# Graph layer on one core: the last node blocks in a new order with any PSUM bank, and the kept units' gathers one in 30 units

## The chip, the cores and the metric

The kernel runs on one core of one Trainium2 chip. The core has five engines with a queue each: TensorE (PE, matmuls into PSUM), VectorE (DVE), ScalarE (ACT), GpSimd (POOL) and SyncE (SP, which here only issues DMAs). The metric is the device time of one execution in microseconds. The kernel before took 2141.97 us as the median of three runs (2139.69 to 2142.32). One more execution was profiled: it took 2142.29 us, and all times of the trace below are of that one. PSUM has eight banks; the kernel calls them pz0 to pz7, and one holds 128 x 512 numbers.

## The reference

A graph layer on 6,250 nodes of 256 features and 206,250 edges of 64 features, sorted by their target node:

```
h    = relu(layernorm(x))                                  # one row per node
e    = relu(raw @ W_e1.T + b_e1) @ W_e2.T + b_e2           # one row per edge
emb  = (e * (clip(pol, 0, 1) + 0.01)) @ W_le.T + b_le
aggr = segment_sum(relu(h[src] + emb), dst)
g    = (h + aggr) @ W_g1.T + b_g1
out  = x + relu(layernorm(g) * ln_g + ln_b) @ W_g2.T + b_g2
```

## The kernel before, in words

**Edges.** W_e2 and W_le are multiplied into one matrix at the start. The edges go in 403 blocks of 512. A block is two *units* of 256 edges, 806 in all (0 to 805), and six blocks are a *group*: 12 units, 68 groups, the last of one block. For one unit PE makes the product with the second matrix (L369) in a bank that ACT has filled with the bias (L399). DVE multiplies by the polarity and adds the gathered rows of h (L754, two instructions), ACT takes the ReLU (L765), and PE sums the rows by target node with a 0/1 matrix as weights (L802). The first layer of a whole group (L335) is made in one stretch after the group's predecessor's last unit: twelve products through the banks, evicted by ACT (L350) and DVE (L347). The sums of a group gather in one bank and are copied to SBUF as `ms` (L820, L822).

**Gathers.** The rows of h come from DRAM by two indirect DMAs for each unit, which POOL issues (L721) into a ring of 25 places. Units 0 to 23 are *kept*: their products were made while h was being computed, and wait in SBUF as `msg`. For units 4 to 23 the gathers are made later and stand between those of other units: `EVERY` (L47) and L705 to L708 say where. Before, unit r's two gathers are ahead of those of unit 24 + 24 (r - 3), so at units 48, 72 and so on to 504. When all 12 units of a kept group have their rows, the group is summed at the end of the running group (24 `msg` matmuls, from `ready` in `add_pairs`, L848), and two node blocks can follow.

**Nodes.** The 6,250 rows are 49 blocks of 128. A block whose groups are done is turned (L173), multiplied by W_g1 (`first`, L188, with the bias added by DVE at L196 or, with `bias_by_pe`, by a one-row matmul, L186), normalised (statistics L158 and L159, square root on ACT L202, reciprocal and scaling L207 and L208), turned again with ReLU on ACT (`second`, L214 and L218), multiplied by W_g2 (`third`, L227), added to x (L232) and stored (L235: SP, and for a last block of 106 rows 10 rows from ACT's queue). Most blocks run beside the edges, a step every unit or two, in a bank that the edges do not use (`Banks.__call__`, L294: `take(False, False)` asks for a bank that last held node work). The sums of groups go to the blocks either through DRAM (`rows_out`, SP, then `far_work`) or, for blocks at the end, by selecting matmuls (L1026, L1045: `node_work`).

**End.** Five blocks are left when the last edge is done. `ending[-2]` (*held*, 128 rows) and `ending[-1]` (the *last*, 106 rows) need the last groups. Three more, the *fillers* (`held_back`, `far_work(..., True)`, L840), could be done before: their rows are summed (L942), but all six steps (`turned`, `one`, `rooted`, `normed`, `two`, `three`) wait for the end, where L1139 to L1168 write the order out by hand. Every engine works its queue in order, so this order decides what waits behind what. A clock gate on PE shows in the profile as the granted clock.

Of the kernel before, what the change touches and what calls it, by code (L numbers as in the profile page):

```python
# [29 lines left out]
L = 6  # L30
# [5 lines left out]
NG = NF + 1  # L36
# [6 lines left out]
RAW = 4  # L43
# [3 lines left out]
EVERY = 24  # L47
SEEDS = 3
FILL = 3
# [51 lines left out]
def gnn_kernel(ctx: ExitStack, tc: tile.TileContext, x, src_c, dst_c, dst_r, pol_c, raw_t, w_e1t, w_e2,  # L101
# [149 lines left out]
    with fast:  # L251
# [22 lines left out]
        class Banks:  # L274

            def __init__(self):
                self.all = [Bank(psz.tile([P, 2, D], F32, name=f"pz{i}")) for i in range(BANKS)]
                self.uses = 0

# [14 lines left out]
            def __call__(self):  # L294
                self.now = self.take(False, False) or self.take(False)
                self.now.reader = self.now.writer = None
                return self.now.tile
# [397 lines left out]
        with tc.tile_pool(name="hg", bufs=1) as hg_p, tc.tile_pool(name="ms", bufs=4) as ms_p, \  # L695
# [9 lines left out]
            for r in range(RAW, KEPT):  # L705
                i = KEPT + EVERY * (r - RAW + 1)
                beside[i] = r
                order.insert(order.index(i), r)  # L708
# [218 lines left out]
            def far_work(w, nd=nd, nh=nh, ab_p=ab_p, filling=False):  # L927
# [37 lines left out]
                def run(i):  # L965
                    stages[i]()
                    if i < len(stages) - 1:
                        at(now + (2, 1, 1, 2, 3)[i], lambda: run(i + 1))
# [5 lines left out]
                if filling:  # L974
                    fillers.append(stages)
                else:
                    at(now + 12, lambda: run(0))
# [10 lines left out]
            def node_work(w, spread_now=False):  # L988
# [82 lines left out]
                ending[gs[-1] - NG].append((sums_of, halves_out, rows_of, one, two, three, gs))  # L1071
# [67 lines left out]
            (held, held_out, held_rows, h_one, h_two, h_three, _), = ending[-2]  # L1139
            (sums_of, halves_out, rows_of, one, two, three, gs), = ending[-1]  # L1140
            f = fillers
            for i in range(FILL):
                f[i][0]()
            held_rows()
            sums_of(gs[:-1])
            add_pairs(last=True)
            f[0][1]()
            h_one()
            sums_of(gs[-1:])
            halves_out()  # L1150
            f[1][1]()
            one()
            for i in range(2):
                f[i][2]()
                f[i][3]()
            f[0][4]()
            h_two()
            f[2][1]()
            f[1][4]()
            f[2][2]()  # L1160
            f[0][5]()
            two()
            f[2][3]()
            h_three()
            f[1][5]()
            three()
            f[2][4]()
            f[2][5]()  # L1168
# [184 lines left out]
```

## Time and profile before

| | us |
|---|---|
| median of three runs | 2141.97 |
| the profiled execution, time | 2142.29 |
| its span, first to last instruction | 2140.6 |
| PE busy | 2095.3 (98%) |
| POOL busy | 1574.8 (74%) |
| DVE busy, ACT busy | 1305.4, 1296.9 (61% each) |
| mean granted clock of PE | 0.994 |

The profile puts 1.69 us of the time outside the span. PE is the engine that is busy nearly throughout; POOL's busy share leaves out the pause between two gathers. In a timeline row stand the start, the length, the engine, the line, the operation with its tiles, the number of instructions merged, and in brackets the idle time ahead of the row and what ended it. The trace counts every float32 matmul of the program twice.

### The profile page before, as it was taken

Reading aid. Unit: us, or ns where it says so; the run is one execution under the profiler, and the core shown is the slowest. Engines: PE = TensorE matmul, PEld = TensorE weight load, DVE = VectorE, ACT = ScalarE, POOL = GpSimd, SP = SyncE. Lnnn points to the kernel's source line nnn. Section 1 sums busy time; section 2 is a strip of 40 time slices with the busy share of each in tenths; the row PEclk is TensorE's granted clock in tenths of the full one; section 3 lists DMA queues with packets and bytes.
Section 4 is the critical chain, followed back from the end, with each engine's and each line's share of the span. In section 5 each row is a group of like instructions: output and inputs, shape, how many; then the busy total and the mean of one; then the engine's idle time right before and its main releaser. Section 6 shows DMA issues by size and latency. Waiting matters only on the chain. (4 is left out here: it accounts for less than half of the span.)

```text
span 2140.6 us, 35567 instructions
## 1 busy us (share of the span) xinstructions
PE 2095.3 (98%) x11940; PEld 1568.3 (73%) x11940; DVE 1305.4 (61%) x2867; ACT 1296.9 (61%) x2392; POOL 1574.8 (74%) x1675
## 2 busy tenths in 40 slices
PE   9999999999999999999999999999999999999997
PEld 6676777677778767777767777777777777777775
DVE  7766566565656666656566565566665666656563
ACT  7655566566656656656656565656665666666662
POOL 6777777777777777777777777777777777777760
PEclk9999999999999999999999999999999999999998
DMA  9545455555555554555555455555455555554550
GB/s 318 192 140 159 147 152 159 148 153 149 158 151 158 155 153 142 158 152 152 154 152 164 136 159 151 161 163 159 142 160 151 158 151 160 157 153 132 155 147 13
DMA packets 143653, 330.48 MB, mean 154 GB/s; under 512 B 35999, under 2 KB 71416, under 8 KB 142712
## 3 DMA queue, kind: packets, MB, share of 16 engines
q0 software_dynamic: 77376, 211.39, 34.5%
q1 hardware_dynamic: 64788, 113.47, 16.4%
q10 hardware_dynamic: 1300, 3.28, 0.4%
q8 instruction: 96, 1.57, 0.3%
q14 instruction: 93, 0.76, 0.1%
HBM read 306.24 MB, written 34.08 MB: 159 GB/s over the span
## 5 line engine op out<-in xcount | busy, mean ns | idle before, releaser
L721 POOL DMA_INDIRECT hg<-hb_d,src_s x1348 | 1286.9, 955 | 412.8 <-issue 246.2
L369 PE MATMUL pz<-wc_s,e 128*128 128x256 f32 x6448 | 1440.9, 380 | 0.2 <-ACT pz L399 0.2
L369 PEld LDWEIGHTS pz<-wc_s,e 128*128 128x128 f32 x6448 | 1212.0, 190 | 189.8 <-issue 28.7
L754 DVE SCALAR_TENSOR_TENSOR hg<-pz,pol_s,hg 128x256 f32<-128x256 f32 x1348 | 594.9, 480 | 593.9 <-PE pz L369 261.1
L765 ACT ACTIVATE hg<-hg 128x512 f32<-128x512 f32 x673 | 423.4, 629 | 502.4 <-DVE hg L754 498.2
L399 ACT ACTIVATE pz<-bc_s 128x512 f32<-128x512 f32 x782 | 453.0, 586 | 0.0
L335 PE MATMUL pz<-raw,we_s 64*128 64x512 f32 x1612 | 381.8, 609 | 25.0 <-DVE hg L754 15.1
L347 DVE TENSOR_SCALAR e<-pz,vecs 128x512 f32<-128x512 f32 x395 | 292.3, 750 | 57.2 <-PE pz L335 25.0
L335 PEld LDWEIGHTS pz<-raw,we_s 64*128 64x128 f32 x1612 | 147.3, 188 | 223.5 <-issue 118.6
L721 POOL DMA_INDIRECT hx<-hb_d,src_s x256 | 243.0, 949 | 78.0 <-issue 52.4
L350 ACT ACTIVATE e<-pz,vecs 128x512 f32<-128x512 f32 x411 | 269.9, 682 | 40.8 <-PE pz L335 35.9
L802 PE MATMUL pz<-hg,sel 128*32 128x256 f32 x2696 | 167.0, 381 | 1.0 <-ACT ms L820 1.0
L802 PEld LDWEIGHTS pz<-hg,sel 128*32 128x32 f32 x2696 | 84.4, 110 | 96.2 <-ACT e L350 44.2
L754 DVE SCALAR_TENSOR_TENSOR hx<-pz,pol_s,hx 128x256 f32<-128x256 f32 x216 | 95.3, 480 | 94.3 <-PE pz L369 36.6
L765 ACT ACTIVATE hx<-hx 128x512 f32<-128x512 f32 x108 | 68.0, 630 | 100.1 <-DVE hx L754 99.9
L736 DVE SCALAR_TENSOR_TENSOR sel<-iota_w,zero_c,rel 128x256 f32<-128x256 f32 x202 | 97.1, 481 | 46.2 <-PE pz L802 46.2
L820 ACT ACTIVATE ms<-pz 128x256 f32<-128x256 f32 x67 | 25.7, 383 | 146.5 <-PE pz L802 144.4
L188 PE MATMUL pz<-wg_s,hT 128*128 128x256 f32 (+1 forms) x176 | 46.5, 387 | 0.0
L227 PE MATMUL pz<-wg_s,nT 128*128 128x256 f32 (+1 forms) x176 | 45.6, 382 | 0.0
L523 POOL TENSOR_TENSOR hb<-xt,rows_b 128x256 f32<-128x256 f32 (+1 forms) x49 | 34.1, 727 | 9.7 <-issue 2.6
L188 PEld LDWEIGHTS pz<-wg_s,hT 128*128 128x128 f32 (+1 forms) x176 | 33.4, 192 | 6.2 <-issue 1.0
L227 PEld LDWEIGHTS pz<-wg_s,nT 128*128 128x128 f32 (+1 forms) x176 | 33.5, 192 | 5.0 <-ACT hT L177 0.4
(135 smaller groups left out, 605.6 us busy)
## 6 DMA issues: line engine op xcount, KB each, us to landing
raw<-in_raw_t_dram SPq DMA_DIRECT2D x99, 512.0 KB
hg<-hb_d,src_s POOLq DMA_INDIRECT x1348
sum_d<-zero_d SPq DMA_DIRECT2D x47, 256.0 KB
ab<-sum_d SPq DMA_DIRECT2D x42, 256.0 KB
sum_d<-ms SPq DMA_DIRECT2D x264, 32.0 KB
hb_d<-hb SPq DMA_DIRECT2D x12, 512.0 KB
xt<-in_x_dram SPq DMA_DIRECT2D x11, 512.0 KB
xt<-in_x_dram SPq DMA_DIRECT2D x43, 128.0 KB
```

The source lines that it names most:

```text
L188: z = nc.tensor.matmul(ph[:n, 0, :], aT[:, c, :n], wg1_s[:, c, :], start=c == 0 and not bias_by_pe, stop=c == 1)
L227: z = nc.tensor.matmul(po[:n, 0, :], nT[:, c, :n], wg2_s[:, c, :], start=c == 0, stop=c == 1)
L335: z[c] = nc.tensor.matmul(bank[s, c].tile.rearrange("p a b -> p (a b)"), we1_s[s * F:(s + 1) * F, c * P:(c + 1) * P], raw[q][s * F:(s + 1) ...
L347: a = nc.vector.tensor_scalar(e1[b][:, c, :], pe, be1_s[:, c:c + 1], 0.0, op0=ALU.add, op1=ALU.max)
L350: a = nc.scalar.activation(e1[b][:, c, :], pe, AF.Relu, bias=be1_s[:, c:c + 1])
L369: z = nc.tensor.matmul(bank.tile[:, i, :], e1[b][:, c, k:k + P], wc_s[:, c, :], start=not seeded and i == c == 0, stop=c == 1, skip_group_ ...
L399: a = nc.scalar.activation(bank.tile, bc_s, AF.Copy)
L721: g = nc.gpsimd.indirect_dma_start(out=hg[u][:, i, :], out_offset=None, in_=hb_d, in_offset=bass.IndirectOffsetOnAxis(ap=src_s[:, 2 * u + ...
L736: nc.vector.scalar_tensor_tensor(sel[g][:, k * S:k * S + n, :], iota_w.rearrange("p (o w) -> p o w", o=1).to_broadcast([P, n, W]), zero_c, ...
L754: product = nc.vector.scalar_tensor_tensor(hg[u][:, i, :], bank.tile[:, i, :], pol_s[:, 2 * u + i:2 * u + i + 1], hg[u][:, i, :], op0=ALU. ...
L765: done[u] = product, nc.scalar.activation(hg[u], hg[u], AF.Relu)
L802: z = nc.tensor.matmul(acc[g][j * W:(j + 1) * W, :], sel[g][:, k * S + j, :], m[:, j % 2, :], start=k == 0, stop=b == blocks_of(g)[-1])
```

## The change

Four things are changed.

1. `EVERY` is 30, and unit r's gathers stand ahead of unit 24 + 30 (r - 4) + 15: at units 39, 69 and so on to 609.
2. The fillers run their first four steps beside the edges, like other blocks; only `two` and `three` are held back.
3. At the end any free bank serves node work (`ps.any`), the one free for longest first.
4. The end's order is written anew. The held block's bias is added by DVE instead of PE, and `one` and the normalising are separate steps, so that the two blocks' can be interleaved.

```diff
-EVERY = 24
+EVERY = 5 * L
...
             def __call__(self):
-                self.now = self.take(False, False) or self.take(False)
+                self.now = None if self.any else self.take(False, False)
+                self.now = self.now or self.take(False)
...
-                i = KEPT + EVERY * (r - RAW + 1)
+                i = KEPT + EVERY * (r - RAW) + EVERY // 2
...
-                    if i < len(stages) - 1:
+                    if i < len(stages) - (3 if filling else 1):
...
                 if filling:
-                    fillers.append(stages)
-                else:
-                    at(now + 12, lambda: run(0))
+                    fillers.append(stages[-2:])
+                at(now + 12, lambda: run(0))
...
                 def one():
-                    box["hs"] = scaled(root(first(box["hT"], gs[-1] >= NG - 2)))
+                    box["hs"] = first(box["hT"], gs[-1] == NG - 1)
+                    if gs[-1] < NG - 2:
+                        normed()
...
+                def normed():
+                    box["hs"] = scaled(root(box["hs"]))
```

The end before and after, as written (`f` and `fillers` are the three held blocks, `h_` the held block of 128 rows):

```
before                          after
f[0][0]() f[1][0]() f[2][0]()   ps.any = True
held_rows()                     fillers[0][0]()   # two
sums_of(gs[:-1])                fillers[1][0]()
add_pairs(last=True)            h_rows()
f[0][1]()                       add_pairs(last=True)
h_one()                         sums_of(gs[:-1])
sums_of(gs[-1:])                fillers[2][0]()
halves_out()                    sums_of(gs[-1:])
f[1][1]()                       halves_out()
one()                           h_one()
f[0][2]() f[0][3]()             one()
f[1][2]() f[1][3]()             normed()
f[0][4]()                       fillers[0][1]()   # three
h_two()                         h_normed()
f[2][1]()                       fillers[1][1]()
f[1][4]()                       two()
f[2][2]()                       fillers[2][1]()
f[0][5]()                       three()
two()                           h_two()
f[2][3]()                       h_three()
h_three()
f[1][5]()
three()
f[2][4]() f[2][5]()
```

**PE, behind the last big sum.** These are PE's first rows after the sum of units 800 to 803 before the change: the three fillers' first turns, then the held block's sums, all in bank pz1 (the number behind a tile's name is its buffer).

```order
L173 MATMUL pz1_139<-ident_64,msg7_119 128x128 x2
L173 MATMUL pz1_139<-ident_64,msg15_127 128x128 x2
L173 MATMUL pz1_139<-ident_64,msg23_135 128x128 x2
L1045 MATMUL pz1_139<-s2_14882,ms_14632 128x128
L1045 MATMUL pz1_139<-s2_14884,ms_14842 128x128
```

At the same place after the change the fillers' second turns stand, the held block's sums follow in a bank of their own, and the last unit's sum stands ahead of the last block's.

```order
L214 MATMUL pz1_139<-ident_64,msg5_117 128x128 x2
L214 MATMUL pz7_145<-ident_64,msg13_125 128x128 x2
L1046 MATMUL pz5_143<-s2_14918,ms_14643 128x128
L1046 MATMUL pz5_143<-s2_14920,ms_14864 128x128
L1046 MATMUL pz5_143<-s2_14922,ms_15052 128x128
L1046 MATMUL pz5_143<-s2_14918,ms_14643 128x128
L1046 MATMUL pz5_143<-s2_14920,ms_14864 128x128
L1046 MATMUL pz5_143<-s2_14922,ms_15052 128x128
L804 MATMUL pz6_144<-hg8_819,sel1_137 32x256 x2
L804 MATMUL pz6_144<-hx2_110,sel1_137 32x256 x2
```

The L173 rows have gone up between the edges' products, one block's L173 and L188 about a group apart.

**ACT, at the very end.** Before, these are ACT's last rows: between turns and roots the ten rows of the last block are stored (L235), and one filler's ReLU stands behind that store.

```order
L202 ACTIVATE rs1_15081<-mv1_15077,eps_t_65 106x1
L202 ACTIVATE msg3_115<-msg4_116,eps_t_65 128x1
L202 ACTIVATE msg11_123<-msg12_124,eps_t_65 128x1
L218 ACTIVATE msg3_115<-pz4_142,vecs_167 128x128 x2
L218 ACTIVATE nT_15097<-pz1_139,vecs_167 128x128 x2
L218 ACTIVATE msg11_123<-pz4_142,vecs_167 128x128 x2
L202 ACTIVATE msg19_131<-msg20_132,eps_t_65 128x1
L218 ACTIVATE nT_15116<-pz0_138,vecs_167 128x106 x2
L235 DMA out_0_dram<-ot_15132 10x256
L218 ACTIVATE msg19_131<-pz4_142,vecs_167 128x128 x2
```

After the change the three fillers' ReLUs come first, two roots are left, and the ReLU behind the store is the held block's (nT_15136).

```order
L218 ACTIVATE msg3_115<-pz1_139,vecs_167 128x128 x2
L218 ACTIVATE msg11_123<-pz7_145,vecs_167 128x128 x2
L822 ACTIVATE ms_15073<-pz6_144 128x256
L218 ACTIVATE msg19_131<-pz4_142,vecs_167 128x128 x2
L202 ACTIVATE rs1_15103<-mv1_15099,eps_t_65 106x1
L202 ACTIVATE rs1_15111<-mv1_15091,eps_t_65 128x1
L218 ACTIVATE nT_15121<-pz6_144,vecs_167 128x106 x2
L235 DMA out_0_dram<-ot_15130 10x256
L218 ACTIVATE nT_15136<-pz4_142,vecs_167 128x128 x2
```

**SP, the held block's loads.** Before, on SP's queue x, the turned x and the row statistics of the held block (L240, L999, L1001) stand between the two pairs of stores of group 65's sums (L906).

```order
L906 DMA sum_d_62<-ms_14842 32x256
L240 DMA xt3_14876<-in_x_dram 128x256
L999 DMA hT_14878<-in_x_t_dram 128x2x128
L1001 DMA stb_14880<-st_d_61 128x256
L906 ISA
L906 DMA sum_d_62<-ms_14842 32x256
```

After the change both pairs of stores are ahead of the three loads.

```order
L908 DMA sum_d_62<-ms_14864 32x256
L908 ISA
L908 DMA sum_d_62<-ms_14864 32x256
L240 DMA xt3_14912<-in_x_dram 128x256
L1000 DMA hT_14914<-in_x_t_dram 128x2x128
L1002 DMA stb_14916<-st_d_61 128x256
```

Elsewhere in PE's queue the sum of the second kept group (the rows L802 with msg12 to msg23) stands behind the first layer that follows unit 515 before and unit 611 after; that of the first (msg0 to msg11) behind unit 227 before and 251 after.

More of the change, by code (lines that the diff above doesn't have):

```diff
@@ L278, in __init__ @@
                 self.uses = 0
+                self.any = False
             def take(self, whole, of=None):
@@ L1070, in node_work @@
                     return lambda: at(now + 2, rows_of)
-                ending[gs[-1] - NG].append((sums_of, halves_out, rows_of, one, two, three, gs))
+                ending[gs[-1] - NG].append((sums_of, halves_out, rows_of, one, normed, two, three, gs))
                 return lambda: None
@@ L1138, in gnn_kernel @@
                 steps.popleft()[1]()
[L1139 to L1144, printed above, removed]
+            (_, _, h_rows, h_one, h_normed, h_two, h_three, _), = ending[-2]
+            (sums_of, halves_out, _, one, normed, two, three, gs), = ending[-1]
+            ps.any = True
+            fillers[0][0]()
+            fillers[1][0]()
+            h_rows()
+            add_pairs(last=True)
             sums_of(gs[:-1])
-            add_pairs(last=True)
-            f[0][1]()
-            h_one()
+            fillers[2][0]()
             sums_of(gs[-1:])
             halves_out()
-            f[1][1]()
+            h_one()
             one()
[L1153 to L1156, printed above, removed]
-            h_two()
[L1158 to L1163, printed above, removed]
+            normed()
+            fillers[0][1]()
+            h_normed()
+            fillers[1][1]()
+            two()
+            fillers[2][1]()
+            three()
+            h_two()
             h_three()
[L1165 to L1168, printed above, removed]
         early.close()
```

## The prediction

> **What bounds the kernel now.** I read the page first, then the waits of PE, then the timelines of PE and POOL around those waits, and last the timelines of all engines behind the last edge. PE is busy for 98% of the span, so only its idle time, or a slower clock, can be won. Between 100 and 1440 us its largest wait is this one; between 1460 and 2100 us no wait of L335 is left.
>
> ```profile
> PE pz L335 <- DVE hg L754: 15.1, 12, 2.3
> L721 POOL DMA_INDIRECT hg<-hb_d,src_s x1348: 942/946/2397, 64.5 to 2081.9; - x193
> ```
>
> PE stands at the first layer of a group because DVE has not freed the banks, and DVE waits for gathered rows. The gathers themselves never pause: 946 ns in the median and 0.30 us between them, from the first to the last. Three windows from the first gather count them, and the rows behind them show two stalls and one group without.
>
> ```profile
> 64.00:976.95 912.95, 692.13 (x724) 1.00 0.51 153
> 64.00:1228.47 1164.47, 882.72 (x924) 1.00 0.51 153
> 64.00:1595.74 1531.74, 1161.03 (x1216) 1.00 0.52 154
> ...
> 976.94 0.94 POOL L721 DMA_INDIRECT hg<-hb_d,src_s  x1 [0.30 <-issue]
> 980.36 4.08 PE L335 MATMUL pz<-raw,we_s 64*128 64x512 f32 x16 [2.13 <-DVE hg L754]
> ...
> 1228.46 0.95 POOL L721 DMA_INDIRECT hg<-hb_d,src_s  x1 [0.31 <-issue]
> 1231.75 4.08 PE L335 MATMUL pz<-raw,we_s 64*128 64x512 f32 x16 [1.99 <-DVE hg L754]
> ...
> 1595.74 0.95 POOL L721 DMA_INDIRECT hg<-hb_d,src_s  x1 [0.30 <-issue]
> 1610.59 5.42 PE L335 MATMUL pz<-raw,we_s 64*128 64x512 f32 x24
> ```
>
> Unit 467 ends a group. Its second gather is number 2 x (444 units + 18 kept ones) = 924, issued at 1228.46, and PE goes on 3.3 us later, at 1231.75. For unit 371 it is number 724, and PE goes on 3.4 us later. So PE gets past the first eight matmuls of L335 at the earliest 3.35 us after the last gather of the running group is issued. For unit 611 (588 units and all 20 kept ones, number 1216) that is 1595.74 + 3.35 = 1599.1. PE got there at 1610.59 + 1.99 (the length of eight such matmuls) = 1612.6, so PE was 13.5 us behind the gathers. The first half of the kernel is paced by the gathers, the second by PE.
>
> Then comes the end. The span closes at 2140.6, 37.7 us after the last large sum (start 2101.80, length 1.07). The PE rows behind it:
>
> ```profile
> 2101.80 1.07 PE L802 MATMUL pz<-hx,sel 128*32 128x256 f32 x16
> 2103.42 0.44 PE L173 MATMUL pz<-ident,msg 128*128 128x128 f32 x2 [0.55 <-DVE ms L822]
> ...
> 2106.15 1.60 PE L1045 MATMUL pz<-s,ms 128*128 128x128 f32 x12 [0.47 <-ACT msg L177]
> 2108.34 1.14 PE L1026 MATMUL pz<-s,ms 128*128 128x106 f32 x8 [0.58 <-DVE hT L1047]
> 2109.41 0.64 PE L802 MATMUL pz<-hg,sel 128*32 128x256 f32 x8
> 2110.55 1.13 PE L188 MATMUL pz<-wg_s,msg 128*128 128x256 f32 x4 [0.50 <-ACT ms L820]
> 2112.20 0.69 PE L186 MATMUL pz<-rows_b,ones 1*128 1x256 f32 x2 [0.52 <-DVE msg L196]
> 2112.82 1.13 PE L188 MATMUL pz<-wg_s,hT 128*128 128x256 f32 x4
> 2113.79 0.59 PE L1026 MATMUL pz<-s,ms 128*128 128x106 f32 x4
> 2115.97 2.08 PE L188 MATMUL pz<-wg_s,msg 128*128 128x256 f32 x4 [1.59 <-DVE hT L1034]
> ...
> 2130.64 1.03 PE L227 MATMUL pz<-wg_s,nT 128*106 128x256 f32 x4
> 2131.50 0.38 PE L214 MATMUL pz<-ident,msg 128*128 128x128 f32 x2
> 2133.72 1.13 PE L227 MATMUL pz<-wg_s,msg 128*128 128x256 f32 x4 [1.84 <-ACTq L1173]
> ```
>
> One bank, pz1, carries nearly every step, so each waits for the reader of the one before (0.47 to 0.58 us each), and from 2115.5 the same L188 takes 2.08 us in place of 1.13: the clock was halved, as the windows below show.
>
> **The change, part by part.** Sums are made against the profiled execution, 2142.29 us, which is 0.32 above the median of 2141.97.
>
> *Gathers.* Up to unit 504 there are now 16 kept gathers instead of 20, so PE stalls less there; but the total is the same again from unit 609. The binding place is therefore unit 611, whose gather keeps number 1216 and its time. Against the 13.5 us stands work that PE had done by then and now has not: the second kept group's sum and the two node blocks that follow it. Their rows (the blocks' steps priced where they stand between edges, by the next row's start):
>
> ```profile
> 1361.83 2.80 PE L802 MATMUL pz<-msg,sel 128*32 128x256 f32 x48
> ...
> 1602.51 0.38 PE L214 MATMUL pz<-ident,hs 128*128 128x128 f32 x2
> 1602.72 5.35 PE L369 MATMUL pz<-wc_s,e 128*128 128x256 f32 x24
> 1607.91 1.03 PE L227 MATMUL pz<-wg_s,nT 128*128 128x256 f32 x4
> 1608.77 1.89 PE L369 MATMUL pz<-wc_s,e 128*128 128x256 f32 x8
> ```
>
> A turn costs 0.21 us and a product 0.86, a block 2 x (0.21 + 0.86) = 2.1, together 2.8 + 2 x 2.1 = 7.0. So PE can be at most 13.5 - 7.0 = 6.5 us earlier at unit 611. The other end is that it is not earlier at all, 0. I take 6.0, near the upper end, because at a gather each 1.25 us the ceiling is known to about half a gather. Behind unit 611 the gathers lead by over 10 us, as they did before, so nothing of it is lost later. Loop: -6.0.
>
> *Fillers' first four steps beside the edges.* PE gets three turns and three products more in the loop, 3 x (0.21 + 0.86) = +3.2. Their DVE and ACT work lies in idle time of both engines, which are busy for 61% of the span. It is an addition, statistics, a scaling, a copy and a root, five short instructions of at most 0.54 us (the L208 row below), so without that cover it costs up to 2.7 us a block, 8 in all.
>
> *SP.* The held block's loads go behind two more stores.
>
> ```profile
> 2053.00 0.60 SPq L1001 DMA_DIRECT2D stb<-st_d  x1
> 2057.27 0.33 DVE L1015 SCALAR_TENSOR_TENSOR hT<-hT,zero_c,stb 128x106 f32<-128x106 f32 x1 [3.27 <-DMA stb<-st_d]
> 2076.66 0.60 SPq L1001 DMA_DIRECT2D stb<-st_d  x1
> 2077.57 3.61 SPq L906 DMA_DIRECT2D sum_d<-ms  x2
> ```
>
> Such a load is there 4.3 us after its issue. The held block's was issued at 2076.66. It now follows the second pair of stores, which ended at 2081.2, so it is there about 5 us later than before, and DVE will stand at its first use for some 2 us, with the L754 of units 797 and 798 behind it. The 3.27 us of such a wait above moved no PE row, so I cost it at 0; without that cover it costs those 2 us.
>
> *The end.* I count from the end of the last large sum (0 is 2102.87 before) and lay the new order out with the rows' durations, back to back by the next row's start. PE waits 0.55 for the copy of the sums, since the first turn takes the sum's bank, as before. Then it has, without a wait because ACT and DVE read other banks meanwhile: two turns 0.76, L1045's 12 matmuls 1.53, the last unit's sum 0.57, L1026's eight 1.07, a turn 0.38, L1026's four 0.55, the held block's L188 0.97, L186 0.62, the last block's L188 1.13. That is at 8.1. The last block's chain follows:
>
> ```profile
> 2115.20 0.54 DVE L208 TENSOR_SCALAR hs<-pz,mv,rs 128x256 f32<-128x256 f32 x1
> ...
> 2131.77 0.42 DVE L232 TENSOR_TENSOR ot<-pz,xt 106x256 f32<-106x256 f32 x1 [0.51 <-PE pz L227]
> 2134.89 0.43 DVE L232 TENSOR_TENSOR msg<-pz,msg 128x256 f32<-128x256 f32 x1 [2.70 <-PE pz L227]
> ...
> 2132.86 0.81 ACT L218 ACTIVATE msg<-pz,vecs 128x128 f32<-128x128 f32 x2 [3.25 <-DVE ot L232]
> ```
>
> From L188's end (2113.95) to the end of L208 (2115.74) it took 1.8, so 9.9; turn 0.44, ReLU 0.85 and L227 1.05 bring 12.3, and meanwhile PE makes the fillers' L227, which are free. L232 0.5 ends at 12.8. Behind it ACT's store and a ReLU, L227 and L232 of one more block, the same chain as before though for another block: from 2132.19 to 2135.32, 3.1. Then the last store, to 2140.6: 5.3. The end is 21.2 us long instead of 37.7: -16.5. PE's one-row L186 of the held block goes (0.62) and a DVE addition of 0.42 comes beside PE's work; both are in this count.
>
> Sum: 2142.29 - 6.0 + 3.2 - 16.5 = **2123.0**.
>
> *The clock.* These windows are 3.41 us long and end where the clock changed:
>
> ```profile
> 2101.88:2105.29 3.41, 1.91 (x21) 0.78 (x21) 1.30 (x3) 1.57 (x4) 0.00 (x0) 1.00 0.00 0
> 2112.12:2115.53 3.41, 2.18 (x10) 1.57 (x10) 1.74 (x7) 0.29 (x1) 0.00 (x0) 1.00 0.00 0
> 2115.53:2118.94 3.41, 2.97 (x6) 1.60 (x6) 1.38 (x5) 0.00 (x0) 0.00 (x0) 0.50 0.00 0
> ```
>
> The clock was halved behind a window with 2.18 us of PE work, 0.62 of it the one-row L186, and not behind one with 1.91. Without L186 the shares are 46% and 56%, so I read the limit as about half a window. In the laid-out end PE has a break of 1.8 us ahead of the last L227 (12.5 to 14.3). A window that holds all of it may have 47% of work, and then the last L227 is 1.1 us longer. The Trainium skill (TensorE: Matmul & The Clock Gate, Part 1) has the clock halved after at least one idle window of about 3.4 us, and advises against PE gaps longer than that. By that rule neither end would lose the clock; this trace disagrees, since its clock fell with a longest gap of 1.59 us just before. By the Trainium skill the sum stays 2123.0, by the rows it may be 2124.1.
>
> **The rivals.** *The loop gives nothing* (15%): the stalls between units 39 and 611 come out as long as before, through stalls early (the first kept gather is now at unit 39, not 48) or breaks of the gathers. Then 2129. For it speaks that gathers up to 2397 ns occur; against it the steady 3.35 us. *The clock falls early in the end* (10%), as at 2115.5: from the held sums on about 5.3 us of back-to-back rows and 2.9 in the last chain double: +8.2, 2131. Against it: every 3.41 us window up to 12.5 has over 80% of PE work. *The gathers have fewer long ones* (10%): 1216 gathers at 1.25 us from 64.5 would be issued by 1585, 11 us before 1595.74; half of that would give 2118. *Slower* (3%): the gathers' pace itself is longer. Since it binds at gather 1216, it decides from (19.3 + 4.3) / 1216 = 19 ns a gather on, 1.27 us instead of 1.25, and then the time is above 2146.6; with 25 ns it is 2153. Nothing in the change touches POOL's work, and the median of 946 ns beside a least of 942 speaks against it. That the fillers do not move is ruled out by the order in PE's queue.
>
> **How the numbers follow.** The forecast, 2123.0 with its own range of 2120 to 2126 (1 us for the ceiling, 1.1 for the clock in the last gap, 1 for rounding over some 20 rows), has 62%, the rivals 15, 10, 10 and 3%. A range from 2118 to 2131 holds all but the far ends, some 85 to 90%. A difference of 0.2%, 4.3 us, is about what a measurement of this kernel can tell from none. Faster by more takes all cases but the slower one and some slack for two rivals at once: 0.94; within it 0.03; slower 0.03.
>
> **What would show it.** Right: stalls of L335 until unit 611 (about 1600 us) instead of 515, in sum some 6 us shorter; L173 of the fillers between edges; the last large sum ends near 2100.1; from there 21 us; no half clock ahead of the last L227. Wrong: a wait of PE behind the held block's load, L214 waiting for other than the sum's copy, stalls of L335 behind unit 611, or the clock at 0.5 while the sums run.

## The result and the profile after

The changed kernel takes 2124.28 us (median of 4 runs, 2123.04 to 2124.77), the kernel before 2142.14 (4 runs, 2139.69 to 2148.03): a ratio of 0.9912, with a 95% interval of 0.9891 to 0.9932. The profiled execution took 2124.57 us against 2142.29. The forecast was 2123.0, with a range of 2118 to 2131.

The page of the changed kernel opens with the span and each engine's busy time:

```profile
span 2122.9 us, 35565 instructions
PE 2087.7 (98%) x11938; PEld 1564.9 (74%) x11938; DVE 1303.5 (61%) x2868; ACT 1298.0 (61%) x2392; POOL 1573.9 (74%) x1675
```

The span is 17.7 us shorter and PE is busy for 7.6 us less, though its work is almost the same: in the kernel before, steps of the end ran at half the clock. Two added lines put the names two lines further down, so L335 is L337 here, L721 is L723, L802 is L804.

The waits of PE from 100 to 1700 us in the changed kernel (total, times, longest):

```profile
PE pz L337 <- DVE hg L756: 9.5, 10, 2.0
PE pz L337 <- DVE hx L756: 4.1, 4, 3.2
```

The same two rows said 15.1 and 2.0 before (hx are four more places of the gathers' ring). So the stalls went from 17.1 to 13.6 us, 3.5 less where some 6 were forecast. The last one is now behind unit 611; here is POOL's row of gather 1216, and PE's rows around it:

```profile
1594.57 0.95 POOL L723 DMA_INDIRECT hg<-hb_d,src_s  x1 [0.30 <-issue]
...
1595.59 1.45 PE L337 MATMUL pz<-raw,we_s 64*128 64x512 f32 x6
1597.81 4.08 PE L337 MATMUL pz<-raw,we_s 64*128 64x512 f32 x16 [0.76 <-DVE hg L756]
1601.82 1.07 PE L804 MATMUL pz<-msg,sel 128*32 128x256 f32 x16
1603.14 1.93 PE L804 MATMUL pz<-msg,sel 128*32 128x256 f32 x32 [0.24 <-DVE sel L738]
1605.60 0.84 PE L804 MATMUL pz<-hg,sel 128*32 128x256 f32 x10 [0.53 <-ACT ms L822]
```

PE goes on 3.24 us after gather 1216 is issued, and is 14.8 us ahead of the kernel before (1612.6 - 1597.8). Then come the moved sum and the two moved node blocks. Five groups later, this is what is left; the first row is of the kernel before, the second of the changed one:

```profile
1764.24 3.27 PE L335 MATMUL pz<-raw,we_s 64*128 64x512 f32 x14
```

```profile
1760.15 3.27 PE L337 MATMUL pz<-raw,we_s 64*128 64x512 f32 x14
```

4.09 us. The same distance holds until unit 767, where the held blocks' first steps begin; they take it down to 0.84 at the last large sum. That sum ends at 2102.0, where 2100.1 was forecast. The rest, 16.9 us, is won in the end, which is 20.9 us long instead of 37.7. PE's rows of it:

```profile
2102.58 0.66 PE L214 MATMUL pz<-ident,msg 128*128 128x128 f32 x4 [0.55 <-DVE ms L824]
2103.07 1.50 PE L1046 MATMUL pz<-s,ms 128*128 128x128 f32 x12
...
2105.07 1.14 PE L1027 MATMUL pz<-s,ms 128*128 128x106 f32 x8
...
2106.70 1.05 PE L188 MATMUL pz<-wg_s,hT 128*128 128x256 f32 x4
2107.68 0.68 PE L186 MATMUL pz<-rows_b,ones 1*106 1x256 f32 x2
2108.28 1.11 PE L188 MATMUL pz<-wg_s,hT 128*106 128x256 f32 x4
2109.23 1.89 PE L227 MATMUL pz<-wg_s,msg 128*128 128x256 f32 x8
2111.31 0.40 PE L214 MATMUL pz<-ident,hs 106*128 106x106 f32 x2 [0.19 <-DVE hs L208]
2111.55 1.05 PE L227 MATMUL pz<-wg_s,msg 128*128 128x256 f32 x4
2112.57 1.11 PE L227 MATMUL pz<-wg_s,nT 128*106 128x256 f32 x4
2113.52 0.38 PE L214 MATMUL pz<-ident,hs 128*128 128x128 f32 x2
2115.68 1.13 PE L227 MATMUL pz<-wg_s,nT 128*128 128x256 f32 x4 [1.78 <-ACTq L1171]
```

Of the long column of brackets of before, three are left. The last one has its reason on ACT's queue: the ten rows' store and the held block's ReLU behind it.

```profile
2114.18 0.59 ACTq L235 DMA_DIRECT2D out_dram<-ot  x1
2114.82 0.81 ACT L218 ACTIVATE nT<-pz,vecs 128x128 f32<-128x128 f32 x2 [2.30 <-DVE ot L232]
```

### The profile page after: what moved, and what is told of

It is laid out like the page before. It is cut to its first block, busy times and chain, and to the rows that moved or that the text cites. A ratio compares the mean times of both kernels' runs of the same rounds, so it can differ in the third digit from the quotient of the medians.

```text
span 2122.9 us, 35565 instructions
## 1 busy us (share of the span) xinstructions
PE 2087.7 (98%) x11938; PEld 1564.9 (74%) x11938; DVE 1303.5 (61%) x2868; ACT 1298.0 (61%) x2392; POOL 1573.9 (74%) x1675
## 3 DMA queue, kind: packets, MB, share of 16 engines
q1 hardware_dynamic: 64788, 113.47, 16.5%
q10 hardware_dynamic: 1300, 3.28, 0.5%
## 5 line engine op out<-in xcount | busy, mean ns | idle before, releaser
L723 POOL DMA_INDIRECT hg<-hb_d,src_s x1350 | 1286.9, 953 | 413.4 <-issue 249.2
L371 PE MATMUL pz<-wc_s,e 128*128 128x256 f32 x6448 | 1441.8, 380 | 0.2 <-ACT pz L401 0.2
L371 PEld LDWEIGHTS pz<-wc_s,e 128*128 128x128 f32 x6448 | 1211.8, 190 | 189.5 <-issue 30.2
L756 DVE SCALAR_TENSOR_TENSOR hg<-pz,pol_s,hg 128x256 f32<-128x256 f32 x1318 | 580.2, 480 | 569.1 <-PE pz L371 239.1
L767 ACT ACTIVATE hg<-hg 128x512 f32<-128x512 f32 x659 | 414.7, 629 | 492.1 <-DVE hg L756 487.2
L337 PE MATMUL pz<-raw,we_s 64*128 64x512 f32 x1612 | 380.6, 608 | 22.1 <-DVE hg L756 9.5
L337 PEld LDWEIGHTS pz<-raw,we_s 64*128 64x128 f32 x1612 | 147.6, 188 | 219.4 <-issue 116.9
L723 POOL DMA_INDIRECT hx<-hb_d,src_s x254 | 242.2, 953 | 77.4 <-issue 48.4
L804 PE MATMUL pz<-hg,sel 128*32 128x256 f32 x2636 | 178.2, 381 | 0.5 <-ACT ms L822 0.5
L756 DVE SCALAR_TENSOR_TENSOR hx<-pz,pol_s,hx 128x256 f32<-128x256 f32 x246 | 108.5, 480 | 114.0 <-PE pz L371 58.4
L804 PEld LDWEIGHTS pz<-hg,sel 128*32 128x32 f32 x2636 | 89.9, 110 | 88.1 <-ACT e L352 38.7
L767 ACT ACTIVATE hx<-hx 128x512 f32<-128x512 f32 x122 | 76.8, 629 | 106.1 <-DVE hx L756 105.7
L822 ACT ACTIVATE ms<-pz 128x256 f32<-128x256 f32 x67 | 25.7, 384 | 144.1 <-PE pz L804 139.0
L804 PE MATMUL pz<-hx,sel 128*32 128x256 f32 x492 | 62.9, 382 | 0.5 <-ACT ms L822 0.5
L227 PE MATMUL pz<-wg_s,nT 128*128 128x256 f32 (+1 forms) x176 | 45.6, 381 | 1.8 <-ACTq L1171 1.8
L188 PE MATMUL pz<-wg_s,hT 128*128 128x256 f32 (+1 forms) x176 | 45.4, 380 | 0.2 <-ACT nT L218 0.2
L227 PEld LDWEIGHTS pz<-wg_s,nT 128*128 128x128 f32 (+1 forms) x176 | 33.0, 189 | 7.6 <-ACTq L1171 2.0
```

The lines of the kernel that those rows point to most:

```text
L188: z = nc.tensor.matmul(ph[:n, 0, :], aT[:, c, :n], wg1_s[:, c, :], start=c == 0 and not bias_by_pe, stop=c == 1)
L227: z = nc.tensor.matmul(po[:n, 0, :], nT[:, c, :n], wg2_s[:, c, :], start=c == 0, stop=c == 1)
L337: z[c] = nc.tensor.matmul(bank[s, c].tile.rearrange("p a b -> p (a b)"), we1_s[s * F:(s + 1) * F, c * P:(c + 1) * P], raw[q][s * F:(s + 1) ...
L371: z = nc.tensor.matmul(bank.tile[:, i, :], e1[b][:, c, k:k + P], wc_s[:, c, :], start=not seeded and i == c == 0, stop=c == 1, skip_group_ ...
L723: g = nc.gpsimd.indirect_dma_start(out=hg[u][:, i, :], out_offset=None, in_=hb_d, in_offset=bass.IndirectOffsetOnAxis(ap=src_s[:, 2 * u + ...
L756: product = nc.vector.scalar_tensor_tensor(hg[u][:, i, :], bank.tile[:, i, :], pol_s[:, 2 * u + i:2 * u + i + 1], hg[u][:, i, :], op0=ALU. ...
```

## The experiments

Each run is one kernel's times and one profiled execution. The runs fell on chips of two kinds. On the chip of one in 36, the held block ahead, the held blocks late and one in 36 together with the held block ahead, the kernel before takes 2143.41 us (7 runs, 2139.93 to 2145.07). On the two slow chips of the other runs it takes 3919.77 (19 runs) and 3993.16 (14 runs), with the same instructions. Its loop waits there for something that the profile doesn't name (last section), so only ends are read from those runs: the time from the end of the last large sum to the end of the span, where the rows have the lengths that they have on the first chip, but for the clock.

**The gathers' places alone** (twice, once on each slow chip):

```diff
-EVERY = 24
+EVERY = 5 * L
...
-                i = KEPT + EVERY * (r - RAW + 1)
+                i = KEPT + EVERY * (r - RAW) + EVERY // 2
```

> The kernel before with the gathers' new places alone. The theory: at unit 611 PE is bound by the gathers, the kept group's sum and two node blocks move behind it, and the loop ends about 4 us earlier (the traces of before and after differ by 4.1 us between units 671 and 767); the end stays as before, 37.7 us from the last large sum. So the last large sum ends near 2098.8, and the profiled time is about 2138. The rival, that the gathers' places change nothing and the 4 us come from the fillers' steps, gives 2142.

> The kernel before with the new places of the kept gathers alone (the run on the slow chip once more). Theory A: PE goes on behind unit 611 3.3 us after gather 1216 is issued, as in the changed kernel, and the moved work takes 10.7 us behind it, so the last large sum ends 4 us earlier relative to that gather than in the kernel before (507.1 us after it there, 503 here); the end has the old order and 36 to 38 us; about 2138 where the kernel before has 2142. Rival B: the gathers' places give the whole of the gain of the loop only together with the end; then no difference.

3890.38 us, ratio 0.9914 (0.9893 to 0.9936), and 3966.51, ratio 0.9940 (0.9921 to 0.9960). They are inconclusive on the loop: PE isn't held at L335 for over 0.12 us anywhere behind 95 us, so no gather binds it there as on the other kind of chip. What they show is the old order's end, 36.2 us long in the one and 42.5 in the other, beside 37.7 in the kernel before on the first chip. PE's rows of the second one show where its clock fell, and behind them stand the windows of 3.41 us ahead of that place and behind it:

```profile
3920.15 0.44 PE L173 MATMUL pz<-ident,msg 128*128 128x128 f32 x2 [0.47 <-ACT msg L177]
3921.06 2.78 PE L1045 MATMUL pz<-s,ms 128*128 128x128 f32 x12 [0.47 <-ACT msg L177]
3924.41 2.04 PE L1026 MATMUL pz<-s,ms 128*128 128x106 f32 x8 [0.58 <-DVE hT L1047]
```

```profile
3917.85:3921.26 3.41, 1.51 (x7) 0.80 (x8) 0.42 (x1) 1.50 (x4) 0.00 (x0) 1.00 0.00 0
3921.26:3924.67 3.41, 2.83 (x13) 2.54 (x13) 0.42 (x1) 0.00 (x0) 0.00 (x0) 0.50 0.00 0
```

L1045's twelve matmuls take 2.78 us instead of 1.60 and L1026's eight 2.04 instead of 1.14: behind the three spaced L173 the clock (the third column from the right) is already halved, 3.5 us into the end (3917.8 to 3921.3), where it fell 12.7 us into it (2102.9 to 2115.5) in the kernel before on the first chip.

**The end alone**, with the gathers at the places of before (also once on each slow chip):

```diff
-EVERY = 5 * L
+EVERY = 24
...
-                i = KEPT + EVERY * (r - RAW) + EVERY // 2
+                i = KEPT + EVERY * (r - RAW + 1)
```

> The changed kernel with the gathers' old places (one in 24 units). The theory: the stalls of L335 up to unit 515 come back with some 17 us in sum, the fillers' steps cost PE 3.2 us in the loop, and the end takes 20.9 us: 2142.3 + 3.2 - 16.8 = 2128.7. If the end's gain needed the later gathers, it would be longer than 21 us here; the rival that the places change nothing gives 2124.5.

> The changed kernel with the gathers' places of before (the run on the slow chip once more): the held blocks' first steps beside the edges and the new end. Theory A: the loop has PE's 3.25 us more, the end is 20.5 to 21 us instead of 37.7, together -13.6: about 2128.5 where the kernel before has 2142. Rival B: in a loop whose PE is not behind, the held blocks' steps find idle time and cost less than 2 us: 2126 to 2127.5.

3901.43 us, ratio 0.9961 (0.9942 to 0.9980), and 3969.80, ratio 0.9944 (0.9926 to 0.9963). Both ends are 20.5 us long, as in the changed kernel (20.9), so the new end doesn't need the new gathers. What the held blocks' steps cost in a loop with the old places can't be told from these chips; that part is inconclusive.

**Node work in its own banks**: the changed kernel without `ps.any = True` (slow chip):

```diff
-            ps.any = True
```

> The changed kernel without any bank for node work at the end: again a bank that last held node work where one is free. If the banks carry part of the end's gain, the fillers' turns, the held block's sums and the last unit's sum wait for each other's readers, 0.4 to 0.9 us in each of four to six places: the end takes 23 to 26 us instead of 20.9, 2127 to 2129. If the order alone carries it, less than 0.5 us is lost: below 2125.

3877.61 us, ratio 0.9905 (0.9867 to 0.9943). The end is 25.7 us long, 5.2 more than the 20.5 of the same end with any bank on the same chip. PE's first rows of it:

```profile
3847.50 0.44 PE L214 MATMUL pz<-ident,msg 128*128 128x128 f32 x2 [0.55 <-DVE ms L824]
3848.84 0.44 PE L214 MATMUL pz<-ident,msg 128*128 128x128 f32 x2 [0.90 <-ACT msg L218]
3850.18 2.93 PE L1046 MATMUL pz<-s,ms 128*128 128x128 f32 x12 [0.90 <-ACT msg L218]
3853.68 0.41 PE L804 MATMUL pz<-hg,sel 128*32 128x256 f32 x2 [0.58 <-DVE hT L1048]
```

In the changed kernel the two L214 stand in one row, L1046 follows it with no wait, and takes 1.50. Here each step waits for the reader of the bank (0.90 + 0.90 + 0.58, and 0.50 and 0.21 in two rows further on, 3.1 in all), and behind these waits the clock is halved (from 3849.9 to 3853.3): L1046 is 1.43 longer. Together 4.5 of the 5.2 us. Without this one line 5.2 us of what the end won (16.9) is lost, and the waits cost more than their own length.

**Filled waits**: the kernel before with 13 matmuls of no use in the two long waits of its end (twice, once on each slow chip).

```diff
+            def spin(k):
+                bank = ps.take(True)
+                for _ in range(k):
+                    nc.tensor.matmul(bank.tile[:, 0, :P], ones, ones, start=True, stop=True)
...
+            spin(6)
...
+            spin(7)
```

> The kernel before with 13 more matmuls of ones (their results are used by nothing) in two gaps of PE at the end, six behind the last block's sums and seven behind its first product; about 0.22 us each, less than the gaps of 1.59 and 2.37 us. If the clock is lost because less than about half of a window of 3.41 us is filled, it now stays at 1.0, the L188 and L227 that took 2.0 and 1.9 us take 1.0 and 0.9, and the end is 4 to 7 us shorter: 2135 to 2138. If the clock falls for another reason, or PE's durations do not set the end, the end stays within 1 us of 37.7: 2142.

> The kernel before with 13 matmuls of no use in the two long waits of its end (the run on the slow chip once more). Theory A: the clock is halved by a stretch of 3.4 us that is less than about half filled, so with both waits filled the steps behind them run at full speed and the end is 32 to 34 us long instead of 37.7, about 2138; unless the clock is already halved by the three first transpositions with their waits of 0.47 us, as on the slow chip, and then the end is 38 us again. Rival B: the halved clock lies beside waits for DVE and ACT and costs the end nothing: 37 us or more with the clock at full all through.

3918.07 us, ratio 0.9987 (0.9972 to 1.0003), and 3990.70, ratio 1.0000 (0.9987 to 1.0013); both ends 38.2 us long. They missed what they were made for: the clock fell ahead of the filled waits, behind the three L173, in both. PE's rows of the second run show the fall and the return:

```profile
3952.90 2.15 PE L1045 MATMUL pz<-s,ms 128*128 128x128 f32 x12 [0.47 <-ACT msg L177]
...
3965.60 2.40 PE L1144 MATMUL pz<-ones 128*128 128x128 f32 x12
3967.84 1.03 PE L188 MATMUL pz<-wg_s,msg 128*128 128x256 f32 x4
```

The clock falls at 3953.8, within L1045; from there to the filler in L1144 all is at half, and behind it L188 is back at 1.03 (2.08 at this place in the kernel before). Three ends of the same code without filler lasted 36.2, 37.7 and 42.5 us, and in them the clock was halved for 10.2, 13.7 and 27.3 us ahead of PE's last row. A straight line through these three, drawn on to no halved clock, comes to about 32.5 us. So an estimate from three executions puts some 5 us of the 37.7 down to the clock. The filler may have helped: with it the clock was halved for 13.7 us in both runs, and in the end of 42.5 us, where it fell at nearly the same place (3.5 us into the end, 3.7 and 4.2 with filler), for 27.3. One execution without filler is too little to show it.

**The kept gathers one in 36 units** (on the chip of the first kind, as are the next three):

```diff
-EVERY = 5 * L
+EVERY = 6 * L
```

> The changed kernel with the kept units' gathers one in 36 units (units 42, 78 and so on to 726) instead of one in 30. Theory A: what the gathers' places can give is a ceiling at the place where the last kept group is summed (unit 611 in the changed kernel): the time of that unit's gather, plus the PE work that has been moved behind it. At unit 731 PE of the kernel before was about 19 us behind the gathers, and 10.7 us of moved work leave some 8 us, against the 4.1 that the changed kernel won; so the last large sum ends about 4 us earlier than in the changed kernel (2098 where that has 2102), the stalls of the first layer sum to 9 or 10 us instead of 13.6 and reach to unit 731, and the end stays 20.9 us long: about 2120 on a chip where the changed kernel takes 2124.3. Rival B: what was missing at unit 611 (4.1 won where 6.0 was forecast) is the pace of the gathers themselves, or stalls early in the kernel that no place of the kept gathers changes; then the last large sum moves by less than 1 us, 2123.5 to 2125. Rival C: the moved work falls into a stretch with other waits, and the time grows by 1 us or more.

2121.99 us (4 runs, 2120.81 to 2123.17), ratio 0.9906 (0.9890 to 0.9923), and a profiled span of 2119.0. In this kernel two small results of a moved node block go to a tile that a held block's first rows are already in (units 756 to 763), so the rows of that held block are not the reference's; the instructions are the same. The last large sum ends at 2098.5, against 2102.0, and the end is 20.5 us long. The stalls are 11.4 us instead of 13.6, more than the 9 or 10 expected, and the last one is behind unit 731, as theory A has it:

```profile
1896.98 0.95 POOL L723 DMA_INDIRECT hg<-hb_d,src_s  x1 [0.30 <-issue]
...
1897.17 1.99 PE L337 MATMUL pz<-raw,we_s 64*128 64x512 f32 x8
1900.26 1.13 PE L337 MATMUL pz<-raw,we_s 64*128 64x512 f32 x4 [1.10 <-DVE hg L756]
```

This is gather 2 x (708 + 20) = 1456, and PE goes on 3.28 us after its issue: the same rule at another gather.

**The held block ahead of the last one's product:**

```diff
-            three()
             h_two()
+            three()
             h_three()
```

> The changed kernel with one line of the end moved: the held block's second transposition (with its ReLU on ACT) ahead of the last block's third product, so that the ReLU no longer stands behind the ten-row store on ACT's queue. Theory A: after the last large sum the changed kernel's path goes through that store (0.59 us) and the ReLU behind it (0.81), with PE standing 1.78 us ahead of its last product; without it PE's last product follows the one before without that wait, and the end takes about 18.9 us instead of 20.9, the time is about 2122.3 where the changed kernel has 2124.3. Rival B: the path ends with the last store whatever ACT does (the last rows' DMA ends last); then the end keeps 20.9 us within 0.3. Rival C: the last block's ReLU and the held block's now meet on ACT and DVE, and the last block's chain is later by as much, so less than 1 us is won.

2124.34 us (4 runs, 2123.01 to 2126.40), ratio 0.9916 (0.9899 to 0.9932): by the median no difference from the changed kernel, where theory A had 2122.3. The trace tells more. POOL's gather 1216, PE's going on, and PE's last row:

```profile
1596.57 0.94 POOL L723 DMA_INDIRECT hg<-hb_d,src_s  x1 [0.30 <-issue]
...
1599.87 1.13 PE L337 MATMUL pz<-raw,we_s 64*128 64x512 f32 x4 [0.89 <-DVE hg L756]
...
2114.71 2.19 PE L227 MATMUL pz<-wg_s,nT 128*106 128x256 f32 x8
```

The wait of 1.78 us ahead of the last L227 is gone, and the end is 18.9 us long, as theory A said. But gather 1216 was issued 2.00 us later than in the changed kernel's profile, PE got past unit 611 2.06 us later, and the last large sum ended 2.06 later. The two cancel. Nothing that this line touches is before the end, so the edit didn't make the gathers later.

**The held blocks' first steps at the end again:**

```diff
-                    if i < len(stages) - (3 if filling else 1):
+                    if i < len(stages) - 1:
...
-                    fillers.append(stages[-2:])
-                at(now + 12, lambda: run(0))
+                    fillers.append(stages)
+                else:
+                    at(now + 12, lambda: run(0))
...
             ps.any = True
+            for k in range(4):
+                for f in fillers:
+                    f[k]()
+            for f in fillers:
+                del f[:4]
```

> The changed kernel with the three held blocks' first four steps back at the end, behind the last large sum, step by step for the three blocks in turn, each step with any free bank. Theory A: these steps cost PE the same wherever PE is busy (3.25 us in the loop of the changed kernel), but at the end they stand on the path with their reads by DVE and ACT: the last large sum ends 3.25 us earlier, the end grows from 20.9 to about 27 us, and the time is 2.5 to 3 us longer, about 2127. Rival B: with any bank the three blocks' chains lie beside each other and beside the held sums, and the end grows only by PE's 3.2 us: no difference, 2124.3. Rival C: PE's waits for the statistics and roots bring the clock down to a half in the end (as in the kernel before at 2115.5), and the end is 32 us or longer, 2132 or more.

2130.15 us (4 runs, 2124.45 to 2131.12), ratio 0.9944 (0.9927 to 0.9961): by the median some 6 us more than the changed kernel, where theory A had 2.5 to 3. The one profiled run is the fastest of the four (2124.45), and its gather 1216 was early:

```profile
1591.78 0.95 POOL L723 DMA_INDIRECT hg<-hb_d,src_s  x1 [0.30 <-issue]
...
2096.63 0.87 PE L173 MATMUL pz<-ident,msg 128*128 128x128 f32 x6 [0.55 <-DVE ms L824]
2097.54 2.86 PE L188 MATMUL pz<-wg_s,msg 128*128 128x256 f32 x12
2102.34 0.96 PE L214 MATMUL pz<-ident,msg 128*128 128x128 f32 x4 [1.94 <-DVE msg L208]
```

With any bank the three turns and products run without a wait, then PE waits 1.94 us for the scaling; the end is 26.6 us long. In the loop the last large sum is 5.95 us earlier than in the changed kernel, 2.7 by the gathers and 3.25 by the steps taken out: what they cost there.

By the intervals of the ratios none of the runs on this chip is told apart from the changed kernel (0.9891 to 0.9932). The profiled executions are compared behind the gather that binds, which leaves out how late the gathers were. From the issue of gather 1216, or of 1456 where that one binds, to the end of the span:

| kernel | gather 1216 issued at | from it to the end | gather 1456 at | from it to the end |
|---|---|---|---|---|
| before | 1595.74 | 544.9 | | |
| changed | 1594.57 | 528.3 | 1895.99 | 226.9 |
| held block ahead | 1596.57 | 526.4 | | |
| held blocks late | 1591.78 | 530.9 | | |
| one in 36 | | | 1896.98 | 222.0 |
| both (36, ahead) | | | 1898.89 | 220.2 |

So the held block ahead gives -1.9 (forecast -2.0) and the held blocks late +2.6 (2.5 to 3). One in 36 gives -4.9 (forecast -4); gather 1456 doesn't bind in the changed kernel, and counted from gather 1216 in both it is -4.4. Each figure is of one execution, but two of them come twice: the held block ahead takes 1.8 from one in 36 as well (222.0 to 220.2), and from gather 1216 to the last large sum's end it is 507.5 us both in the changed kernel and with the held block ahead. The other three runs of the held blocks late lie higher than 2127 (2129.28 to 2131.12). They have no trace; their mean clocks, 0.995, 0.995 and 0.997 beside 0.997 in the profiled one, name no cause, and why stays open.

**Both, one in 36 and the held block ahead** (the same block's rows as with one in 36 are not the reference's):

> Both of the edits before that are forecast to win: kept gathers one in 36 units, and the held block's second transposition ahead of the last block's third product. Theory A: the one acts up to unit 731 and the other behind the last large sum, so they add up: the last large sum ends near 2098, the end takes about 18.9 us, and the time is about 2118 where the changed kernel has 2124.3. Rival B: only one of the two gives what it should (see those two runs); then 2120 to 2122.5.

2120.60 us (4 runs, 2119.98 to 2121.24), ratio 0.9898 (0.9881 to 0.9914), the shortest time of all. That is 2.6 us more than theory A's 2118 and lies in rival B's range, though both edits gave what they should. Behind gather 1456 it is 6.7 us shorter than the changed kernel (226.9 - 220.2), by the spans 3.8 (2119.1 against 2122.9), since its gathers were 2.9 us later in the profiled execution. Its end is 18.7 us long.

**One in 35, and the held block ahead** (the edit to `h_two` above beside this one), with the moved blocks done before the held ones begin:

```diff
-EVERY = 5 * L
+EVERY = 35
```

> The changed kernel with the kept units' gathers one in 35 units (units 41, 76 and so on to 706, so that the last kept group is summed behind unit 707, and its two node blocks are done before the held blocks begin) and the held block's second transposition ahead of the last block's third product. Theory A: as with one in 36, PE is held by the gathers up to the place where the last kept group is summed, here behind number 2 x (684 + 20) = 1408 at unit 707, and goes on 3.3 us after its issue; the stalls end there, all moved work comes behind it, and the end is 18.8 us long. The span's end minus the issue of that gather is then the same as in the run with one in 36 and the same end, within 1 us of 220.2 + 60.3 (24 units of PE work) = 280.5, and the time is 2119.5 to 2122, beside 2124.3 of the changed kernel. Rival B: between units 707 and 731 the gathers are faster than PE, so that the earlier place costs the most part of what one in 36 won: 2122 to 2124.

This run fell on a slow chip: 3955.48 us, ratio 0.9904 (0.9886 to 0.9923). Its end is 18.8 us long, as expected. Whether the loop gives what one in 36 gave can't be seen there, so it isn't shown that this version beats the changed kernel on a chip of the first kind.

## Why the prediction was right, point by point

- **The binding place and the ceiling.** Right. PE goes on 3.24 us after gather 1216 (forecast 3.35), no stall comes behind it, and the kernels on the same kind of chip show the like: 3.30 with the held block ahead, 3.34 with the held blocks late, and 3.28 behind gather 1456 with one in 36. The gather itself came 1.2 us earlier than before, which the forecast had as unchanged. That was luck: with the held block ahead, the same kernel up to there, it came 0.8 later than before.
- **What the loop gives: -6.0 forecast, -4.1 measured.** The step that was off is the term for the work that had been moved behind unit 611: 7.0 in the forecast, 14.8 - 4.1 = 10.7 in the trace. The forecast took each moved instruction's own length. By the starts of all rows of these five groups beside before's, the sum took 3.8 (2.8, waits of 0.24 and 0.53, and the way back to the edges), the two blocks 4.8, the edges' products (L371) between their steps 1.5 more than before, and the rest of the first layer 0.6. The trace of before had most of that price: the stretch of four groups with the second kept group's work in it, beside the next four groups without it (length, then the busy time of PE, PEld, DVE, ACT and POOL).

```profile
1354.74:1488.10 133.36, 130.82 (x781) 97.66 (x780) 81.04 (x179) 80.54 (x152) 101.07 (x107) 1.00 0.54 160
1488.10:1610.59 122.49, 122.49 (x709) 92.98 (x709) 74.45 (x159) 75.89 (x139) 92.84 (x98) 1.00 0.52 155
```

  The first is 10.9 us longer, of which 1.1 is the stall behind unit 515: 9.8. With it the ceiling is 13.5 - 9.8 = 3.7. The 4.1 measured holds 1.2 us of the early gather, and without that it would be 2.9. With the held block ahead, where the loop is the same, the gather came 0.8 later than before's and the last large sum ended 1.2 later: there the loop gave 2.0, and the held blocks' steps cost their 3.25.
- **The held blocks' steps beside the edges: +3.2 forecast, +3.25 measured**, three times 1.08, each of them a step in the distance to the kernel before. PE's own part makes up all of it, so DVE's and ACT's part cost nothing there. At the end the same steps cost 5.7 us (26.6 against 20.9).
- **SP.** Right. The load is late and DVE waits for it, 2.62 us where 2 were forecast, and no row of PE moves. DVE's row in the changed kernel:

```profile
2084.72 0.35 DVE L1016 SCALAR_TENSOR_TENSOR hT<-hT,zero_c,stb 128x128 f32<-128x128 f32 x1 [2.62 <-DMA stb<-st_d]
```

- **The end: 21.2 us forecast, 20.9 measured.** Right in its order too: the wait of 0.55 for the copy, then PE without a wait to the last block's L188, then the last block's chain, and the held block's behind the ten rows' store. L188 ends at 7.4 us (forecast 8.1), the last addition at 15.2 (15.9), and what follows took 5.6 (5.3). That the path goes through ACT's store is shown by the run in which it doesn't: 18.9.
- **Any bank.** The forecast counted no wait because the readers use other banks; without the line the end is 5.2 us longer. Of the 16.9 us that the end won, the runs give this line 5.2 and the steps taken out 5.7. No run splits the rest, some 6 us, between the new order and the clock, and the clock has a part in the 5.2 too.
- **The clock.** No half clock between the last large sum and the end of PE's last row (the last L227, 1.13 us), and none there in any of the eight profiles with any bank, this one among them; behind that row it falls in all of them. In the old ends it was halved ahead of that row for stretches of 3.41, 6.83, 13.65 and 27.31 us, whole multiples of 3.41, which is why the windows here have that length. The forecast's limit, about half a window of PE work, doesn't hold as a rule. The window that ended where the clock fell held 1.51 us of PE work in one run (44%), but 1.99 (58%) in this one, of the second run with filled waits, more than the 1.91 (56%) that did no harm in the kernel before:

```profile
3950.38:3953.79 3.41, 1.99 (x14) 1.29 (x13) 0.00 (x0) 1.15 (x3) 0.00 (x0) 1.00 0.00 0
```

  Busy time alone doesn't decide it. The rule of the Trainium skill (TensorE: Matmul & The Clock Gate, Part 1), which halves the clock after at least one idle window of about 3.4 us, isn't borne out either if idle means a window without work: no wait in that window is longer than 0.47 us. The same section has the window run freely, so that its place differs from one execution to another; the falls at 3.5 and 12.7 us into the same end agree with that.
- **The rivals.** That the loop gives nothing, or that the clock falls early, didn't come. The gathers do vary: in the profile of the changed kernel they gave 1.2 us, and with the held blocks late 4.0, where the rival had 5.

So the sum by the traces is -4.1 + 3.25 - 16.9 = -17.7, the forecast -6.0 + 3.2 - 16.5 = -19.3. The end's new length came as laid out; the term that was mis-sized is the moved work, and the early gather covered a part of it.

## What to carry to other kernels

A bunch of work that was moved cost more here than its own instructions (10.7 us against 7.0): price it by the stretch that holds it against a like stretch without it, which the trace of before shows. Where a paced engine holds the busy one up to a certain place, the time up to that place varies with the pace, and an edit behind it is read from that place on, not from the whole time. In this tail of short dependent steps, a bank for each step saved the waits for its readers, and the clock stayed whole.

## What was not expected of the hardware

- On two chips the same program took 1.83 and 1.86 times as long (3919.77 and 3993.16 us for the kernel before, against 2142.14). The page of the last kernel above, and two of the largest waits of DVE from 100 to 3900 us:

```profile
PE 2436.5 (62%) x11938; PEld 1775.2 (45%) x11938; DVE 1293.8 (33%) x2868; ACT 1289.1 (33%) x2392; POOL 1566.0 (40%) x1675
```

```profile
DVE hg L756 <- issue: 896.1, 103, 24.5
DVE hg L756 <- remote: 635.3, 36, 23.4
```

  DVE, ACT and POOL are busy for as long as on the other kind of chip, and DVE stands still for up to 24.5 us at a time, waiting for nothing that the profile names. From 100 to 3900 us it has 128 pauses of over 6 us, 1935 us in sum, which is about the time that is lost; in the changed kernel on the other kind of chip none is over 3.4 us. Most of POOL's gathers (1319 of 1576) are issued within these pauses. What holds DVE isn't shown. PE is busy for 2436.5 us instead of 2087.7, at a granted clock of 0.78 in the mean.
- The issue of gather 1216 differs by 4.8 us between the four executions of the table (1591.78 to 1596.57), 4 ns a gather. The earliest and the latest are of one chip, and the two kernels are the same up to there. Where it binds, the whole time moves with it by up to 0.2%, more than some of the edits give.
- The old end lasted 36.2, 37.7 and 42.5 us in three executions of the same code, and the clock was halved for 10.2, 13.7 and 27.3 us of them; the new one lasted 20.5 to 20.9 us in four.
